# A scan of line convolutions: border products with 96 weight columns, side by side, and another order of products

## The chip, the cores and the metric

The kernel runs on one core of one Trainium2 chip. The metric is the device time of one execution in microseconds (us). A core has five engines that run side by side: TensorE (PE in the profile; its weight loads are listed apart as PEld), VectorE (DVE), ScalarE (ACT), GpSimd (POOL) and SyncE (SP), which here issues most of the DMA transfers.

## What is computed

The input x has 32 images of 48 channels, 64 rows and 128 columns, in float32. Two layers are applied, each `x = x + scan(groupnorm(x))`. The scan goes over the image four times: down the rows, up the rows, right over the columns, left over the columns. Each of its steps takes the line before it, convolves it along the line with 5 taps (48 channels to 48), adds a bias and adds the result to the line at hand:

```
def step(w, b):
    def f(carry, inp):
        nxt = inp + _conv1d(carry, w, b)   # 5 taps, padding 2
        return (nxt, nxt)
    return f
...
x = x + _L0_conv_ref(_gn(x), ...)
x = x + _L1_conv_ref(_gn(x), ...)
```

Each step needs the one before it. Group normalisation uses 16 groups of 3 channels over the whole image.

## The kernel before

**Layout.** A line is cut into blocks of 8 positions. A block has 8 x 48 = 384 values, channel by position, which lie on partitions as three groups of 128: group 0 holds positions 0, 1 and two thirds of 2; group 1 the rest of 2, then 3, 4 and a third of 5; group 2 the rest of 5, then 6 and 7. The table `PIECES` (line 50) tells where each piece lies: position, first and last channel, group, first partition. The free dimension holds block and image: 8 images at a time, 16 blocks in a row of 128 (128 columns of data). In a column scan two groups of images are taken together, again 128 columns.

**A step** (`step`, line 664) is nine products, listed in `PRODUCTS` (line 63) as input group, output group, and shift by a block. Seven stay in the block. Two are border products: (2, 0, -1) takes the last positions of the block before into group 0, and (0, 2, 1) the first positions of the block after into group 2. Their data is shorter by a block: 120 columns in a row scan, 112 in a column scan. Every product uses a 128 x 128 piece of the weight tile. Each of the three output groups has its own PSUM tile with one buffer; as soon as its last product is issued, a `scalar_tensor_tensor` on VectorE (line 684) adds the bias and the input line and writes the new line, which the next step's products read. A float32 product is two weight loads and two matmuls for TensorE.

**Phases.** `PHASES` (line 75) is the order of work: eight row phases of 126 steps (63 down, 63 up), one for each layer and group of 8 images, and four column phases of 254 steps (127 right, 127 left), each for two groups: 2024 steps in all. Row results go to DRAM (`ups`, by `move_rows`, line 528) and come back as columns (`load_unit`, line 572), in quarters of the width. A column phase of layer 0 adds the residual, keeps the result in DRAM and gathers statistics for the next layer; one of layer 1 adds the residual, permutes and stores the output, three quarters of it by way of the DRAM tiles `held` (`hold_result`, `let_result`, line 658).

**What sets the order.** Nothing is left to a scheduler: `in_order` chains the instructions of each engine in the order of the program. An agenda (`at`, `spread`) holds all side work with a due step, and `catch_up` emits what is due ahead of each step. On an engine's queue, side work therefore stands between steps. SP's queue holds nearly all transfers (line 200) and runs ahead of the steps where nothing makes it wait.

**Weights.** `load_weights` (line 232) puts the five taps in DRAM (`taps`), clears the weight tile and fills it with one transfer for each of the ten pieces, 5 x 48 columns wide. It is called six times: once in the first group's work, and at steps 176 and 180, 556, 1188 and 1192 by the agenda, whose transfers SP issues earlier.

**The start.** `first_group` (line 955) is written out by hand: loads of the first images in two parts, `take(0, b)` and `take(1, b)`, two transfers each; between them `let_go(n)` releases n of the transfers that were held back (an identity, the weights, masks and biases). The statistics of the last part lead to the scale of the first rows and so to the first step.

Of the kernel before, what the change touches and what calls it, by code (L numbers as in the profile page):

```python
# [33 lines left out]
C = 48  # L34
ODD = 64
P = ODD + C
TAPS = 5
# [5 lines left out]
E8 = 8  # L43
FULL = 128
NG = E8 * C // FULL
# [4 lines left out]
PIECES = (  # L50
    (0, 0, 48, 0, 0),
    (1, 0, 48, 0, 48),
    (2, 0, 32, 0, 96),
    (2, 32, 48, 1, 0),
    (3, 0, 48, 1, 16),
    (4, 0, 48, 1, 64),
    (5, 0, 16, 1, 112),
    (5, 16, 48, 2, 0),
    (6, 0, 48, 2, 32),
    (7, 0, 48, 2, 80),  # L60
)

PRODUCTS = (
    (0, 0, 0),
    (0, 1, 0),
    (1, 0, 0),
    (1, 1, 0),
    (2, 0, -1),
    (2, 1, 0),
    (1, 2, 0),  # L70
    (0, 2, 1),
    (2, 2, 0),
)

PHASES = (
    ("rows", 0, 0),
# [15 lines left out]
def kernel(  # L92
# [11 lines left out]
    NH = H // E8  # L104
# [29 lines left out]
    def const(shape, name):  # L134
# [9 lines left out]
    wt = {  # L144
        k: early[:, i * WEIGHTS : (i + 1) * WEIGHTS].rearrange("p (i n) -> p i n", i=NG)
        for i, k in enumerate(("down0", "down1", "right"))
    }
# [51 lines left out]
    def dma(dst, src, queue=None):  # L199
        (queue or nc.sync).dma_start(dst, src)  # L200
# [31 lines left out]
    def load_weights(key: str, layer: int, way: int, dma=dma):  # L232


        t = taps[layer][way]
        for j in range(TAPS):
            d, si = divmod(TAPS - 1 - j, 2)
            dma(t[:, j], w[SIDES[si], layer, way, d, SIDES[0]])
        nc.gpsimd.memset(wt[key], 0.0)
        for e, c0, c1, i, p0 in PIECES:  # L240
            to = C * (e - TAPS // 2) - FULL * (i - 1)
            dma(
                wt[key][p0 : p0 + c1 - c0, i, to : to + TAPS * C],
                t[c0:c1].rearrange("c k m -> c (k m)"),
            )

    def load_constants(dma):
# [391 lines left out]
    def in_output(j, g, e):  # L639


        t = out[g * GB : (g + 1) * GB].rearrange("b c (a e) w -> e (c a) b w", e=E8)
        return t[e, :, :, j * WQ : (j + 1) * WQ]
# [14 lines left out]
    def let_result(j, half, e):  # L658

        src = held[j, half].rearrange("o p (a b n) -> (o p a) b n", a=NH, b=GB)  # L660
        dma(in_output(j, half, e), src[e * C * NH : (e + 1) * C * NH])


    def step(key, weights, b_at, src, inp, dst, whole, part):


        ps = [
            ps_step.tile([FULL, N], F32, tag=f"step{o}", name=f"step{o}_{key}")
            for o in range(NG)
        ]  # L670
        left = [sum(1 for p in PRODUCTS if p[1] == o) for o in range(NG)]
        seen = [0] * NG
        for i, o, s in PRODUCTS:
            seen[o] += 1
            nc.tensor.matmul(  # L675
                part(whole(ps[o]), -s),
                weights[:, i, FULL * (o - NG * s - i + 1) : FULL * (o - NG * s - i + 2)],
                part(src(i), s),
                start=seen[o] == 1,
                stop=seen[o] == left[o],  # L680
            )
            if seen[o] == left[o]:
                layer, way = b_at
                nc.vector.scalar_tensor_tensor(  # L684
                    dst(o),
                    whole(ps[o]),
                    bd[:, o, layer, way : way + 1],
                    inp(o),
                    ALU.add,
                    ALU.add,  # L690
                )

    def row_step(k, h, prev, inp, name):
        _, layer, g = PHASES[k]

        def part(t, s):
            return t[:, max(0, s) * GB : N + min(0, s) * GB]

        step(
            f"{layer}{g}{name}{h}",  # L700
            wt[f"down{layer}"],
            (layer, DOWN),
            lambda i: prev[:, i],
            lambda o: inp[:, o],
            lambda o: row(k, h)[:, o],
            lambda ps: ps,
            part,
        )

    def col_step(k, way, v0, v1):  # L710
        _, layer, pair = PHASES[k]

        def col(v):
            kb, e = divmod(v, E8)
            j, kk = divmod(kb, KQ)
            view = slot[slots(k)[j % 3]].rearrange(
                "p (o m e k b) -> p o e k m b", o=NG, e=E8, k=KQ, b=GB
            )
            return lambda o: view[:, o, e, kk]

        def part(t, s):
            t = t.rearrange("p (s a) b -> p s a b", s=2)
            return t[:, :, max(0, s) : NH + min(0, s)] if s else t

        step(
            f"{layer}{pair}{'drl'[way]}{v1}",
            wt["right" if way == RIGHT else "left"],
            (layer, way),
            col(v0),
            col(v1),  # L730
            col(v1),
            lambda ps: ps.rearrange("p (m b) -> p m b", b=GB),
            part,
        )
# [87 lines left out]
    def plan_cols(k, t0, prev):  # L822
# [83 lines left out]
        if layer and not final:  # L906
            todo = [(j, half, e) for j in HELD for half in range(2) for e in range(E8)]
            for n, what in enumerate(todo):
                at(end + 63 + 1.9 * n, let_result, *what)
# [35 lines left out]
    def more_weights(key, layer, way):  # L945
        load_weights(key, layer, way)
# [8 lines left out]
    def first_group():  # L955
# [5 lines left out]
        def let_go(n):  # L961
            for _ in range(min(n, len(later))):
                dma(*later.pop(0))
# [18 lines left out]
        for b in range(2 * GB):  # L982
# [3 lines left out]
            i, b = divmod(b, GB)  # L986
            (nc.vector if b % 2 else nc.gpsimd).memset(parts[i][32:64, b], 0.0)

        def take(i, b):
            for s in range(2):  # L990
                take_batch(0, b, i * HALF + s * rows, s, parts[i])
# [15 lines left out]
        def rows_by_product(h0, n):  # L1007
            src = parts[0][0:C].rearrange("p b (r k e) -> p e r k b", k=NK, e=E8)
            for o in range(NG):
                ps = ps_rows.tile([FULL, n * N], F32, tag=f"rows{o}", name=f"rows{o}_{h0}")  # L1010
                mine = [(e, m) for m, (e, _, _, g, _) in zip(to_row, PIECES) if g == o]
                for i, (e, m) in enumerate(mine):
                    nc.tensor.matmul(
                        ps.rearrange("p (r k b) -> p r k b", r=n, b=GB),
                        m,
                        src[:, e, h0 : h0 + n],
                        start=i == 0,
                        stop=i == len(mine) - 1,
                    )
                nc.scalar.copy(  # L1020
                    row_views(0)[0][:, o, h0 : h0 + n],
                    ps.rearrange("p (r n) -> p r n", n=N),
                )
# [3 lines left out]
        for b in range(1, 3):  # L1027
            take(0, b)
        load_weights("down0", 0, DOWN, hold)
        load_constants(hold)  # L1030
        for b in range(3, GB):
            let_go(3)
            take(0, b)
        for b in range(4):
            let_go(3)
            take(1, b)
        for b in range(GB):
            stats.take(0, parts[0], b)
# [3 lines left out]
            put_row(0, r)  # L1042
        for b in range(4, GB):
            take(1, b)
            let_go(5)
        rows_by_product(0, 4)
        rows_by_product(4, 4)
        for r in range(12, 16):
# [32 lines left out]
        take_in(1, 0, nats1[0])  # L1081

    in_order(first_group)
    at(starts[0] + 10, scale_rows, 0, 40, 48)
    for j in range(1, 4):
# [71 lines left out]
```

## Time and profile before

| what | value |
|---|---|
| median of 3 runs | 4360.81 us (4360.26 to 4363.12) |
| span of the profiled execution, its own time | 4362.4 us |
| TensorE matmul / weight load busy | 4148.9 us / 4119.6 us |
| VectorE / ScalarE / GpSimd busy | 2178.5 / 1337.5 / 887.7 us |
| matmuls, weight loads | 36624 each |
| DMA moved | 680.34 MB in 2112607 packets |
| first step's first weight load | 96.6 us |
| last matmul ends | 4283.2 us |

A line of the groups reads: line of the kernel, engine, operation, written tile <- read tiles, shapes, count | busy us, mean ns of one | idle time of the engine before them and what ended it. A line of the time line reads: start in us, length in us, engine, line, operation, tiles, shapes, count, and in brackets the idle time before it. A line of the stretches reads: from and to in us, length, then the busy time and count on TensorE, weight load, VectorE, ScalarE and GpSimd, then the granted TensorE clock, the mean busy share of the 16 DMA engines (overlapping packets can bring it above 1) and GB/s. The shape `128*112` behind a matmul or weight load is rows of the array by weight columns; a matmul's `128x112` is its data.

### The profile page before, as it was taken

Reading aid. Unit: us, or ns where it says so; the run is one execution under the profiler, and the core shown is the slowest. Engines: PE = TensorE matmul, PEld = TensorE weight load, DVE = VectorE, ACT = ScalarE, POOL = GpSimd, SP = SyncE. Lnnn points to the kernel's source line nnn. Section 1 sums busy time; section 2 is a strip of 40 time slices with the busy share of each in tenths; the row PEclk is TensorE's granted clock in tenths of the full one; section 3 lists DMA queues with packets and bytes.
Section 4 is the critical chain, followed back from the end, with each engine's and each line's share of the span. In section 5 each row is a group of like instructions: output and inputs, shape, how many; then the busy total and the mean of one; then the engine's idle time right before and its main releaser. Section 6 shows DMA issues by size and latency. Waiting matters only on the chain. (4 is left out here: it accounts for less than half of the span.)

```text
span 4362.4 us, 90034 instructions
## 1 busy us (share of the span) xinstructions
PE 4148.9 (95%) x36624; PEld 4119.6 (94%) x36624; DVE 2178.5 (50%) x6554; ACT 1337.5 (31%) x2656; POOL 887.7 (20%) x859
## 2 busy tenths in 40 slices
PE   4898999998999999999999999999999999999992
PEld 2898999998999999999999999999999999999992
DVE  6344444446665444444446665444444444444443
ACT  2583301435795545100006774503000012110122
POOL 4561011324322020010004310000000024410352
PEclk9999999999999999999999999999999999999996
DMA  9999799866998989579407989839288049999999
GB/s 191 171 192 163 111 155 164 217 128 198 231 200 149 157 160 157 91 127 195 85 1 239 227 166 141 127 59 163 37 140 184 1 82 245 236 240 156 172 199 180
DMA packets 2112607, 680.34 MB, mean 156 GB/s; under 512 B 2000448, under 2 KB 2052032, under 8 KB 2072256
## 3 DMA queue, kind: packets, MB, share of 16 engines
q1 hardware_dynamic: 2014176, 582.29, 70.3%
q10 hardware_dynamic: 94816, 86.00, 9.7%
q0 software_dynamic: 3200, 6.30, 0.6%
q8 instruction: 288, 4.72, 0.5%
q14 instruction: 127, 1.04, 0.1%
HBM read 397.57 MB, written 295.99 MB: 159 GB/s over the span
## 5 line engine op out<-in xcount | busy, mean ns | idle before, releaser
L553 ACT ACTIVATE arena<-arena,offset,scale 128x256 f32<-128x256 f32 (+2 forms) x816 | 577.0, 801 | 413.5 <-DMA arena<-mid 160.9
L612 POOL TENSOR_TENSOR arena<-arena 128x2048 f32<-128x2048 f32 x80 | 362.8, 4550 | 1504.4 <-PE step_10l L675 452.9
L510 POOL COPY arena<-arena 112x256 f32<-112x256 f32 x458 | 271.1, 653 | 553.3 <-DMA arena<-in_x 298.9
L675 PE MATMUL step_00r<-arena,early 128*128 128x128 f32 x2286 | 259.0, 277 | 15.4 <-DMA arena<-upa 15.2
L675 PEld LDWEIGHTS step_00r<-arena,early 128*128 128x128 f32 x2286 | 258.3, 194 | 16.1 <-issue 15.5
L675 PE MATMUL step_01r<-arena,early 128*128 128x128 f32 x2286 | 258.5, 277 | 14.3 <-DMA arena<-upa 14.3
L675 PEld LDWEIGHTS step_01r<-arena,early 128*128 128x128 f32 x2286 | 258.1, 193 | 14.7 <-issue 14.4
L675 PE MATMUL step_11r<-arena,early 128*128 128x128 f32 x2286 | 258.5, 276 | 5.9 <-DVE arena L684 5.9
L675 PEld LDWEIGHTS step_11r<-arena,early 128*128 128x128 f32 x2286 | 257.8, 193 | 6.5 <-DVE arena L684 6.2
L444 ACT ACTIVATE early<-arena 128x256 f32<-128x256 f32 x192 | 129.3, 674 | 426.8 <-PE step_01l L675 328.7
L675 PE MATMUL step_00l<-arena,wleft 128*128 128x128 f32 x2286 | 257.9, 276 | 0.0
L675 PEld LDWEIGHTS step_00l<-arena,wleft 128*128 128x128 f32 x2286 | 257.5, 193 | 0.0
L675 PE MATMUL step_10r<-arena,early 128*128 128x128 f32 x2286 | 256.1, 275 | 0.0
L675 PEld LDWEIGHTS step_10r<-arena,early 128*128 128x128 f32 x2286 | 255.7, 192 | 0.3
L675 PE MATMUL step_11l<-arena,wleft 128*128 128x128 f32 x2286 | 255.8, 275 | 0.0
L675 PEld LDWEIGHTS step_11l<-arena,wleft 128*128 128x128 f32 x2286 | 255.5, 192 | 0.2 <-DVE arena L684 0.2
L675 PE MATMUL step_01l<-arena,wleft 128*128 128x128 f32 x2286 | 255.7, 275 | 0.0
L675 PEld LDWEIGHTS step_01l<-arena,wleft 128*128 128x128 f32 x2286 | 255.5, 192 | 0.1
L675 PE MATMUL step_10l<-arena,wleft 128*128 128x128 f32 x2286 | 255.5, 275 | 0.0
L675 PEld LDWEIGHTS step_10l<-arena,wleft 128*128 128x128 f32 x2286 | 255.4, 192 | 0.0
L637 ACT COPY arena<-arena 128x256 f32<-128x256 f32 x172 | 99.5, 656 | 414.0 <-POOL arena L612 166.7
L377 ACT ACTIVATE early<-arena 112x512 f32<-112x512 f32 x192 | 121.1, 631 | 298.2 <-DMA arena<-in_x 227.2
(176 smaller groups left out, 7117.1 us busy)
## 6 DMA issues: line engine op xcount, KB each, us to landing
arena<-in_x SPq DMA_DIRECT2D x48, 768.0 KB, 12.8
xin<-arena SPq DMA_DIRECT2D x96, 384.0 KB, 5.5
arena<-xin SPq DMA_DIRECT2D x96, 384.0 KB, 8.1
mid<-arena SPq DMA_DIRECT2D x96, 384.0 KB, 7.8
arena<-mid SPq DMA_DIRECT2D x192, 192.0 KB, 4.4
upb<-arena SPq DMA_DIRECT2D x192, 192.0 KB, 3.9
arena<-upb SPq DMA_DIRECT2D x96, 384.0 KB, 11.9
arena<-xin SPq DMA_DIRECT2D x186, 192.0 KB, 4.3
```

Source lines behind the costliest of these rows:

```text
L377: nc.scalar.activation(junk[0:P], piece, AF.Identity, accum_out=self.sum[:, at[0], at[1]],)
L444: nc.scalar.activation(junk[:, 0:n], view[:, b], AF.Identity, accum_out=self.sum[:, i, j : j + 1])
L510: copy(dst[:, r, q], src[:, r0 + r, q])
L553: nc.scalar.activation(args[0], args[0], AF.Identity, bias=args[2], scale=args[1])
L612: eng.tensor_tensor(unit, unit, nat, ALU.add)
L637: copy(by_w(perm)[:, a], src[:, a])
L675: nc.tensor.matmul(part(whole(ps[o]), -s), weights[:, i, FULL * (o - NG * s - i + 1) : FULL * (o - NG * s - i + 2)], part(src(i), s), star ...
```

## The change

Group 2 now holds positions 6 and 7 on partitions 0 to 95 and the two thirds of position 5 behind them. What a border product writes then lies on the first 96 partitions in both directions (positions 0 and 1 of group 0, 6 and 7 of group 2), and it uses 96 weight columns and the first 96 partitions of its PSUM tile. The two border products are the third and fourth of a step, and the order of the others is different. As the positions of group 2 are no longer in ascending order, a piece's weights aren't one run of columns: `weight_runs` works the runs out, 25 in place of 10, with a transfer for each. The results of positions 2 and 5 are let go in two transfers each, where one served: 60 in place of 48. At the start, `let_go` releases 4 and 7 transfers at a time in place of 3 and 5.

```diff
-    (5, 16, 48, 2, 0),
-    (6, 0, 48, 2, 32),
-    (7, 0, 48, 2, 80),
+    (6, 0, 48, 2, 0),
+    (7, 0, 48, 2, 48),
+    (5, 16, 48, 2, 96),
 )
 PRODUCTS = (
     (0, 0, 0),
+    (2, 2, 0),
+    (0, 2, 1),
+    (2, 0, -1),
+    (1, 0, 0),
+    (1, 2, 0),
     (0, 1, 0),
-    (1, 0, 0),
     (1, 1, 0),
-    (2, 0, -1),
     (2, 1, 0),
-    (1, 2, 0),
-    (0, 2, 1),
-    (2, 2, 0),
 )
+BORDER = 2 * C
+def weight_runs():
+    runs = []
+    for e, c0, c1, i, p0 in PIECES:
+        mine = []
+        for tap in range(TAPS):
+            t, q = divmod(e + tap - TAPS // 2, E8)
+            for qe, m0, m1, g, q0 in sorted(PIECES):
+                if qe == q:
+                    mine.append((tap * C + m0, FULL * (g + NG * t - i + 1) + q0, m1 - m0))
+        at, to, n = mine[0]
+        for a, b, m in mine[1:]:
+            if (a, b) == (at + n, to + n):
+                n += m
+            else:
+                runs.append((c0, c1, i, p0, at, to, n))
+                at, to, n = a, b, m
+        runs.append((c0, c1, i, p0, at, to, n))
+    return runs
+WEIGHT_RUNS = weight_runs()
@@ load_weights
-        for e, c0, c1, i, p0 in PIECES:
-            to = C * (e - TAPS // 2) - FULL * (i - 1)
+        for c0, c1, i, p0, at, to, n in WEIGHT_RUNS:
             dma(
-                wt[key][p0 : p0 + c1 - c0, i, to : to + TAPS * C],
-                t[c0:c1].rearrange("c k m -> c (k m)"),
+                wt[key][p0 : p0 + c1 - c0, i, to : to + n],
+                t[c0:c1].rearrange("c k m -> c (k m)")[:, at : at + n],
             )
@@ let_result
-        dma(in_output(j, half, e), src[e * C * NH : (e + 1) * C * NH])
+        for n, c0, c1, g, p0 in PIECES:
+            if n == e:
+                at = (g * FULL + p0) * NH
+                dma(in_output(j, half, e)[c0 * NH : c1 * NH], src[at : at + (c1 - c0) * NH])
@@ step
             seen[o] += 1
+            m = BORDER if s else FULL
+            at = FULL * (o - NG * s - i + 1)
             nc.tensor.matmul(
-                part(whole(ps[o]), -s),
-                weights[:, i, FULL * (o - NG * s - i + 1) : FULL * (o - NG * s - i + 2)],
+                part(whole(ps[o])[0:m], -s),
+                weights[:, i, at : at + m],
                 part(src(i), s),
@@ first_group
         for b in range(3, GB):
-            let_go(3)
+            let_go(4)
             take(0, b)
         for b in range(4):
-            let_go(3)
+            let_go(4)
             take(1, b)
...
             take(1, b)
-            let_go(5)
+            let_go(7)
```

## The prediction

> **What bounds the kernel now.** I read the page's shares first, then groups with shapes kept apart in an undisturbed stretch (700 to 900 us), then time lines around the few matmuls that are shaped otherwise, then the waits that interrupt the steps.
>
> ```profile
> span 4362.4 us, 90034 instructions
> PE 4148.9 (95%) x36624; PEld 4119.6 (94%) x36624; DVE 2178.5 (50%) x6554; ACT 1337.5 (31%) x2656; POOL 887.7 (20%) x859
> ...
> L675 PEld LDWEIGHTS step_00r<-arena,early 128*128 128x128 f32 x1785 | 199.7, 192 | 0.6 <-DVE arena L684 0.3
> L675 PE MATMUL step_00r<-arena,early 128*128 128x128 f32 x1390 | 191.1, 277 | 0.1
> L675 PE MATMUL step_00r<-arena,early 128*128 128x112 f32 x396 | 74.0, 268 | 0.0
> ```
>
> TensorE is never idle there. A product is two weight loads and two matmuls, a step has nine products: 18 pairs. 200 us / 1785 loads = 112 ns per load; the single records of the trace say 111.7 ns from load to load, without exception, and the median step is 18 x 111.7 = 2010 ns. 2024 steps x 2.010 = 4068 us; the rest is 96.6 us before the first step, 79 us after the last and 118 us of interruptions.
>
> Who sets 111.7, the load or the matmul? The border matmuls stream 112 columns in a column scan (120 in a row scan). In the single records the matmul behind one starts after 98 ns (105 in rows) instead of 112, then waits: the next load comes after 111.7 all the same. So around a border product the weight load binds, at 128 columns. Does a narrower load take less? The group averages answer:
>
> ```profile
> 1302.55 0.68 PEld L272 LDWEIGHTS ps_r<-mv_r_r,mask_in 128*112 128x112 f32 x6
> 1303.14 0.97 PEld L675 LDWEIGHTS step_02d<-arena,early 128*128 128x128 f32 x8
> ...
> 1307.16 0.75 PEld L276 LDWEIGHTS ps_r<-mean_c_r,maskp 112*128 112x128 f32 x6
> 1307.84 0.30 PEld L675 LDWEIGHTS step_02d<-arena,early 128*128 128x128 f32 x2
> ```
>
> Six loads of 112 weight columns take 0.59 us until the next line's load, six of 128 take 0.68. Singly: 98.3 against 111.7 ns, 13.4 ns for 16 columns, 0.84 ns a column. An estimate for 96 columns from these two: 98.3 - 13.4 = 84.9 ns. The first of the six still took 110 ns, since the matmul before it had 128 columns. A load begins when the previous pair's matmul begins; so the time from one load to the next is the longer of this load and the matmul of the pair before it.
>
> **The change, part by part.** *Border products with 96 columns, side by side.* Take the pairs X (full), b1, b2, b3, b4 (two border products), Y (full). After b1's load: 84.9 against X's matmul of 111.7, so 111.7. After b2, b3, b4: 84.9 against a border matmul of 98.3 (105 in rows), so 98.3 (105). After Y: 111.7 against 98.3, so 111.7. Three intervals of 18 shrink: 3 x 13.4 = 40.2 ns per column step, 3 x 6.7 = 20.1 per row step. Apart, each border product would give one interval. Bounds: nothing, if 96 columns load like 128; four intervals (53.6 and 26.8), if Y's load also starts early. I take three, by the group-average rows.
>
> A rule would give far more: the Trainium skill, "TensorE: Matmul & The Clock Gate", section "Back-to-back issue gap", has an isolated matmul occupy N/2.4 + 2.5 ns, 49 ns for 112 columns. Then loads alone would bind: four intervals x 26.8 = 107 ns a step, 217 us in all, about 4144 us. The row here is 98 ns from one float32 matmul's start to the next; the measurement decides, and I stay with 40.2 and 20.1.
>
> *Order of products.* Output groups now end after products 5 (group 0), 6 (group 2) and 9 (group 1) and are first read by products 1, 2 and 5 of the next step. Before: 5, 6, 9, where the group of 6 had to be out of its PSUM tile by product 2. The distances are the same, four products each, only the last has two border products inside it.
>
> ```profile
> 1012.38 0.61 DVE L684 SCALAR_TENSOR_TENSOR arena<-step_00l,bd,arena 128x128 f32<-128x128 f32 x2 [0.75 <-PE step_00l L675]
> 1013.28 0.35 DVE L684 SCALAR_TENSOR_TENSOR arena<-step_00l,bd,arena 128x128 f32<-128x128 f32 x1 [0.30 <-PE step_00l L675]
> ```
>
> From the last matmul's start 314 ns to VectorE's start, 350 of work, 50 to the waiting load: 714 ns, where eight intervals and a little (896) are there. Measured over all steps the median slack is 193, 157 and 182 ns for the three results; the last falls to 182 - 40 = 142. No wait, so zero; without that cover each missing ns would come back 2024 times.
>
> *Moved partitions.* Ten pieces and ten transfers per group as before: zero in all stores and loads, which SP issues. Two exceptions. A weight load needs 25 transfers in place of 10, six times, and letting the held results go needs 60 in place of 48: 102 more on SP's queue, at 0.45 us by
>
> ```profile
> 472.37 4.50 SPq L200 DMA_DIRECT2D early<-taps  x10
> ```
>
> 46 us of issue if nothing covered it. Later it is covered: behind the weights of 472 and 492 us SP next waits for rows from VectorE (27.2 us of waiting from 498 to 560); behind those of 2584 its loads are due some 60 steps later; the held results end at 4058, the next store goes out at 4099. At the start it is not: 15 more stand ahead of the last image (`let_go` 4 and 7 for 3 and 5), and its statistics lead the first step.
>
> ```profile
> 0.00:100.00 100.00, 43.44 (x70) 18.65 (x71) 66.89 (x100) 17.60 (x35) 41.55 (x65) 1.00 0.97 188
> ```
>
> The DMA share (0.97) is full; packets of 960 B took 100 ns, of 192 B 33 ns, so 624 more packets add about 0.7 us on 16 engines and 15 completions 0.3: lower bound 1 us. Upper: 15 x 0.45 = 7 us if SP is the limit. SP mostly waits for earlier images here (29.9 us), so nearer the lower: +2.5.
>
> *What the saving meets.* It doesn't arrive where something else ends the wait.
>
> ```profile
> L684 DVE SCALAR_TENSOR_TENSOR arena<-step_01d,bd,arena 128x128 f32<-128x128 f32 x9 | 3.0, 349 | 17.2 <-DMA arena<-xin 14.3 <-PE step_01d L675 2.1 <-ACT arena L553 0.8
> ...
> 3899.05 0.35 DVE L684 SCALAR_TENSOR_TENSOR arena<-step_11r,bd,arena 128x128 f32<-128x128 f32 x1 [6.55 <-DMA arena<-upb]
> ...
> 4220.00:4260.00 40.00, 39.96 (x357) 39.77 (x357) 19.14 (x60) 10.13 (x18) 25.90 (x17) 1.00 1.21 188
> 4260.00:4300.00 40.00, 23.22 (x208) 23.02 (x207) 23.67 (x45) 8.55 (x15) 18.52 (x17) 0.82 1.24 191
> ```
>
> Step 142 waits at 422 us for rows that the DMA engines, full since the start, bring: the first 142 row steps give nothing. At 3899 (step 1834) the third quarter is late, its loads released at step 1801: 33 x 40 ns = 1.3 us more waiting. From 4100 on (step 1933) the DMA share stays above 1.1 to the end: the last 91 column steps give nothing. Around step 540 ScalarE's scaled rows come 2 to 4 us ahead with the DMA full; from 451 the steps gain 3.2: 1.0 us lost.
>
> Sum: (1016 - 91) x 40.2 = 37.2 us; (1008 - 142) x 20.1 = 17.4; together 54.6. Against it 2.5 + 1.3 + 1.0 = 4.8. Profile: 4362.4 - 49.8 = 4312.6. The profiled span lies 1.6 above the median of the runs (4360.8), so **4311**.
>
> **Rivals.** *Four intervals* (0.09): the records show a load 16 ns behind its matmul's start after a border, so some slack is passed on; 54.6/3 = 18.2 more, 4293. Against: the load spacing never moved from 111.7. *Two intervals, or DMA takes a third back* (0.09): 4329; for it, the DMA share is above 0.95 in over a third of the 100 us stretches; against, late data stops the steps only at 16, 32, 142 and 1834. *Nothing* (0.08): 96 columns load like 128; 4361 + 2.5 = 4363. Against: 98.3 for 112. *Slower* (0.08): the array drains whenever the number of active columns changes. The Trainium skill, "TensorEngine Tiling (Array Packing)", section "Key Properties", says that changing the tiling mode drains TensorE; 112 columns still reach into the fourth 32, 96 do not, so the row that shows no drain between 112 and 128 (98 ns into the full load at 1303.14) doesn't exclude it. A drain bares what a 275 ns matmul hides, 163 ns, twice a step: 326 - 30, x 2024, near 4960 us; from some 13 ns per change on it decides. [...]
>
> **How the numbers follow.** The likeliest case (0.66) is 4311, its own range 4302 (start and losses near zero, part of the first 142 steps kept) to 4323 (start 7, one later weight load uncovered). The range adds four intervals below and two above: 4290 to 4342, holding 0.66 + 0.09 + 0.09, less a little. About 0.2% (8.7 us) can be told from no change. Faster: 0.66 + 0.18 = 0.84, of which I keep 0.83; same 0.08; slower 0.09.
>
> **What would show it.** Right: load spacings of 98 and 105 three times a step, steps of 1970 and 1990 ns; loads of 96 columns near 165 ns; first step near 99 us; the wait at step 142 longer by about 2 us, at 1834 by 1; a tail longer by 3 to 4. Wrong: spacings of 111.7 (nothing), above 112 (drain), or VectorE waits at the head of each step.

## The result, and the profile after

The changed kernel takes 4321.68 us (median of 4 runs, 4318.79 to 4327.19), the kernel before 4361.97 us beside it (4 runs, 4360.26 to 4368.4): a ratio of 0.9906, 95% interval 0.9892 to 0.992. The forecast was 4311 with a range of 4290 to 4342: the direction and the range held, and 40.3 us came where 49.8 were worked out. The small gap hides two larger ones, one on each side.

The head of the page of the changed kernel:

```profile
span 4325.4 us, 89999 instructions
...
PE 4072.9 (94%) x36624; PEld 4042.5 (93%) x36624; DVE 2177.4 (50%) x6554; ACT 1337.2 (31%) x2656; POOL 891.9 (21%) x859
```

The number of matmuls and loads is the same, and TensorE's busy time fell by 76 us, twice as much as the span (37.0 us). So the steps gained more than the span shows, and idle time grew. Both halves can be read. First the steps: groups of weight loads and matmuls with shapes kept apart, from 2000 to 2200 us. In the kernel before there is one group of loads:

```profile
L675 PEld LDWEIGHTS step_01r<-arena,early 128*128 128x128 f32 x1788 | 200.0, 192 | 0.2
```

and in the changed kernel:

```profile
L706 PEld LDWEIGHTS step_01r<-arena,early 128*128 128x128 f32 x1431 | 167.9, 192 | 0.0
L706 PEld LDWEIGHTS step_01r<-arena,early 128*96 128x96 f32 x408 | 47.4, 164 | 0.0
L706 PE MATMUL step_01r<-arena,early 128*128 128x128 f32 x1432 | 178.1, 276 | 0.0
L706 PE MATMUL step_01r<-arena,early 128*96 128x112 f32 x408 | 55.8, 259 | 0.0
```

Loads of 96 columns last 164 ns from issue to end, where those of 128 last 192; there is no idle time between them. The count gives the step: 1839 loads in 200 us, where the kernel before has 1788. From the single records the median step is 1960 ns in column scans and 1980 in row scans, before 2010 in both. The saving is 50 and 30 ns a step, forecast 40.2 and 20.1: 1016 x 50 + 1008 x 30 = 81.0 us over the whole kernel, where 61.1 would have followed from the forecast's figures.

Then the idle time. I split each profiled execution at the first step's first load and into the scans' phases, and took the time above "number of steps x the phase's median step" as waiting (us):

| part | before | after | more |
|---|---|---|---|
| up to the first step | 96.6 | 109.1 | 12.5 |
| waits, steps 0 to 505 (three phases) | 78.3 | 82.6 | 4.3 |
| waits, fourth phase, from step 506 | 5.3 | 17.8 | 12.5 |
| waits, eighth phase, from step 1138 | 5.1 | 12.8 | 7.7 |
| waits, last phase | 9.6 | 11.8 | 2.2 |
| waits, other phases | 20.1 | 19.9 | -0.2 |
| after the last step | 79.2 | 84.3 | 5.1 |
| sum | | | 44.1 |

81.0 - 44.1 = 36.9 us, against 37.0 between the two spans. More than half of the step time won is given back in waits here. The profiled execution is the slowest of the changed kernel's four, 5.5 us above their median; by the medians 40.3 of the 81.0 us came through, so about half was given back.

The two largest have their lines. In the stretches of the start, 60 to 80 us, the DMA share (the figure before the last) is 0.98 with the kernel before and 0.82 with the changed one:

```profile
60.00:80.00 20.00, 14.31 (x16) 4.29 (x14) 11.22 (x20) 3.04 (x4) 10.86 (x26) 1.00 0.98 212
```

```profile
60.00:80.00 20.00, 19.06 (x21) 5.89 (x20) 8.53 (x15) 2.65 (x5) 10.86 (x26) 1.00 0.82 188
```

In the fourth phase, the time line of SP's queue, of ScalarE and of VectorE in the changed kernel:

```profile
1325.13 12.48 SPq L227 DMA_DIRECT2D early<-taps  x25
...
1342.80 2.84 SPq L227 DMA_DIRECT2D arena<-in_x  x2
...
1358.89 0.63 ACT L403 ACTIVATE early<-arena 112x512 f32<-112x512 f32 x1 [21.07 <-DMA arena<-in_x]
...
1371.83 0.21 ACT L344 ACTIVATE std_r<-var_r 128x24 f32<-128x24 f32 x1
...
1372.07 0.30 DVE L348 RECIPROCAL std_r<-std_r 128x24 f32<-128x24 f32 x1 [9.85 <-ACT std_r L344]
```

and the same stretch in the kernel before:

```profile
1327.76 4.75 SPq L200 DMA_DIRECT2D early<-taps  x10
...
1339.75 1.19 SPq L200 DMA_DIRECT2D arena<-in_x  x2
...
1353.24 0.63 ACT L377 ACTIVATE early<-arena 112x512 f32<-112x512 f32 x1 [13.52 <-DMA arena<-in_x]
...
1366.18 0.20 ACT L318 ACTIVATE std_r<-var_r 128x24 f32<-128x24 f32 x1
...
1366.63 0.29 DVE L322 RECIPROCAL std_r<-std_r 128x24 f32<-128x24 f32 x1
```

Read from top to bottom: 25 weight transfers hold SP's queue 12.48 us in place of 4.75; the images behind them go out 3.05 us later, though the weights began 2.6 us earlier; ScalarE's sixteen passes over these images begin 5.65 us later; the standard deviation that VectorE's row normalisation wants stands on ScalarE behind those sixteen, so VectorE waits 9.85 us, and with it the `scalar_tensor_tensor` whose line the next step's matmuls need. Step 591 starts 9.6 us late. In the kernel before the same deviation was ready 0.25 us ahead of its use (1366.38 against 1366.63 us): there was hardly a margin, and nothing in a table of busy shares says so.

### The profile page after: what moved, and what is told of

Read it like the earlier page. It is cut to its first block, busy times and chain, and to the rows that moved or that the text cites. A ratio compares the mean times of both kernels' runs of the same rounds, so it can differ in the third digit from the quotient of the medians.

```text
span 4325.4 us, 89999 instructions
## 1 busy us (share of the span) xinstructions
PE 4072.9 (94%) x36624; PEld 4042.5 (93%) x36624; DVE 2177.4 (50%) x6554; ACT 1337.2 (31%) x2656; POOL 891.9 (21%) x859
## 5 line engine op out<-in xcount | busy, mean ns | idle before, releaser
L706 PE MATMUL step_00r<-arena,early 128*128 128x128 f32 x2286 | 252.4, 274 | 15.3 <-DMA arena<-upa 14.2
L706 PEld LDWEIGHTS step_00r<-arena,early 128*128 128x128 f32 x2286 | 251.9, 187 | 15.8 <-issue 15.8
```

What stands on the lines that cost most here:

```text
L706: nc.tensor.matmul(part(whole(ps[o])[0:m], -s), weights[:, i, at : at + m], part(src(i), s), start=seen[o] == 1, stop=seen[o] == left[o],)
```

## The experiments

Two questions were open. Does the step follow the rule "the longer of this load and the matmul of the pair before", with only its figures off? And do the waits come from the extra transfers, or from steps that now run ahead of what feeds them? Beside these four kernels the kernel before took 4361.06 us (median of 7 runs, 4353.1 to 4367.38).

**All new pieces, transfers and orders, but loads of 128 columns.**

```
-BORDER = 2 * C
+BORDER = FULL
```

> The changed kernel with 128 weight columns again in the border products (side by side, new order, new pieces and transfers all kept). Theory (narrow loads give the gain): steps of 2010 ns, no shorter interval; the time is the changed kernel's plus its 50 x 1016 + 30 x 1008 ns = 81 us, less what the waits give back, 4375 to 4403, above the kernel before by the new transfers alone. Rival (order or neighbourhood gives the gain): near 4322.

Measured: 4378.55 us (4372.95 to 4382.47), ratio 1.0042, interval 1.0027 to 1.0057: slower than before by 17.5 us. Groups from 2000 to 2200 us:

```profile
L706 PEld LDWEIGHTS step_01r<-arena,early 128*128 128x128 f32 x1792 | 200.2, 192 | 0.0
L706 PE MATMUL step_01r<-arena,early 128*128 128x128 f32 x1393 | 173.4, 276 | 0.0
L706 PE MATMUL step_01r<-arena,early 128*128 128x112 f32 x400 | 59.6, 272 | 0.0
```

The steps are back at 2010 ns in both scans, with 1792 loads in 200 us. So standing side by side and the other order are worth nothing alone; the 96 columns are the whole gain, and what the change brings besides costs 17.5 us in the medians. The profiled execution, the fastest of its four, shows 8.8 us of them: first step at 103.4 (+6.8), fourth phase +11.4, the first three phases -5.5, the end -3.5, each other phase between -1.1 and +0.9. At step 591 the same chain stands:

```profile
1331.44 12.84 SPq L227 DMA_DIRECT2D early<-taps  x25
...
1365.09 0.63 ACT L403 ACTIVATE early<-arena 112x512 f32<-112x512 f32 x1 [21.24 <-DMA arena<-in_x]
...
1378.26 0.30 DVE L348 RECIPROCAL std_r<-std_r 128x24 f32<-128x24 f32 x1 [8.86 <-ACT std_r L344]
```

No step is faster here, and step 591 is still 8.6 us late. In the three kernels below, all with 25 transfers at this place, it is 6.8 to 9.9 us late, and in the kernel before not at all. So the wait does not come from steps that run ahead. That the longer turn of the weights on SP's queue makes it is read from the lines; a kernel with all else changed but 10 transfers here was not run.

**The two border products apart.**

```
 PRODUCTS = (
     (0, 0, 0),
+    (2, 0, -1),
     (2, 2, 0),
     (0, 2, 1),
-    (2, 0, -1),
     (1, 0, 0),
```

> The changed kernel with the second and third product swapped in the list so that a full product stands between the two border products, 96 columns kept. Theory (an interval is the longer of a load and of the matmul of the pair before): each border product alone has one short interval, not three for two: steps of about 1974 (columns) and 1987 ns (rows), 22 us more than the changed kernel, near 4343. Rival (each narrow load gains by itself): steps stay at 1960 and 1980, near 4322.

The edit moves the fourth product of the changed kernel to the second place, which puts (2, 2, 0) between the two border products. Measured: 4326.72 us (4318.62 to 4328.09), ratio 0.992, interval 0.9906 to 0.9935; steps of 1973 ns in column scans and 1987 in row scans. Its loads from 2000 to 2200 us, 1826 for the changed kernel's 1839:

```profile
L706 PEld LDWEIGHTS step_01r<-arena,early 128*128 128x128 f32 x1421 | 174.6, 192 | 0.0
L706 PEld LDWEIGHTS step_01r<-arena,early 128*96 128x96 f32 x405 | 55.5, 164 | 0.0
```

The intervals from load to load in the records around each border product are 110.7, 95.9, 110.0 (columns) and 110.7, 102.4, 110.0 (rows), all others 111.7: one short interval for a border product that stands alone, three for two that stand together, as the rule has it. The steps cost 1016 x 13 + 1008 x 7 = 20.3 us more than in the changed kernel, the medians differ by 5.0, and the ranges overlap. In the profiled executions, this kernel's fastest against the changed kernel's slowest, the one with the products apart is even the shorter by 8.7 us: its first step came 6.3 us earlier, its waits were 18.3 us fewer, its end 4.3 us shorter. So the steps show what standing together wins, but the times of the two kernels can't be told apart; by the medians three quarters of it are lost in waits.

**Border loads of 112 columns, side by side.**

```
-BORDER = 2 * C
+BORDER = 112
```

> The changed kernel with 112 weight columns in the border products. Theory: a load of 112 columns takes 98.3 ns, longer than the column scan's matmul (96.0) and shorter than the row scan's (102.7): column steps near 1967, row steps unchanged at 1980 ns, 7 us more than the changed kernel, near 4329. Rival (loads alone set the interval): rows grow as well; other rival (anything under 128 is the same): near 4322.

Measured: 4325.6 us (4319.56 to 4327.71), ratio 0.9919, interval 0.9905 to 0.9934; steps of 1968 and 1980 ns. Its groups from 2000 to 2200 us:

```profile
L706 PEld LDWEIGHTS step_01r<-arena,early 128*112 128x112 f32 x404 | 48.9, 178 | 0.0
...
L706 PE MATMUL step_01r<-arena,early 128*112 128x112 f32 x404 | 56.0, 261 | 0.0
```

In column scans the short intervals are 96.7, 98.3 and 98.3 ns, where the changed kernel has 95.9, 95.9 and 95.8. So with 112 columns the load binds (98.3, as the small loads of the kernel before had it), and with 96 columns the matmul binds: 95.9 ns for 112 data columns. In row scans, with 120 data columns, both kernels have 102 to 103: the matmul binds in either. This separates the two terms that the forecast had set equal. Narrowing the load below 112 columns wins 8 ns a column step and nothing in rows.

**The 25 weight transfers of the start on ScalarE's queue.** The held transfers carry their queue with them, and those left to SP are let go in the rounds of the kernel before.

```
             dma(
                 wt[key][p0 : p0 + c1 - c0, i, to : to + n],
                 t[c0:c1].rearrange("c k m -> c (k m)")[:, at : at + n],
+                nc.scalar if key == "down0" else None,
             )
...
-            let_go(4)
+            let_go(3)
...
-            let_go(7)
+            let_go(5)
```

> The changed kernel with the first weights' 25 transfers issued from ScalarE's queue and the held transfers let go by 3 and 5 as before. Theory (the 15 extra transfers take SP's turns ahead of the images): first step at 96 to 99 us instead of 109, about 10 to 12 us less in all, near 4310. Rival (the DMA engines are full, it doesn't matter who issues): first step stays above 105, near 4321.

Measured: 4319.67 us (4313.58 to 4321.92), ratio 0.9905, interval 0.9888 to 0.9922, not to be told from the changed kernel; first step at 106.6 us. The stretches of its start and ScalarE's queue:

```profile
40.00:60.00 20.00, 18.90 (x22) 6.15 (x21) 5.32 (x9) 7.21 (x12) 4.66 (x8) 1.00 0.60 106
60.00:80.00 20.00, 16.96 (x19) 5.21 (x17) 10.29 (x18) 3.04 (x4) 8.54 (x15) 1.00 1.02 233
```

```profile
33.39 18.67 ACTq L227 DMA_DIRECT2D early<-taps  x25
```

```profile
SPq L227 <- DMA early<-taps: 8.1, 6, 4.6
```

From 60 to 80 us the DMA engines are full again, but from 40 to 60 their share is only 0.60. ScalarE issues 25 transfers in one go of 18.67 us, and SP itself waits 8.1 us for six of them: a transfer on the other queue still holds up SP here. The loss moved 20 us forward and stayed. My expectation of a start like the kernel before's was wrong; the rival's numbers came (above 105, near 4321), but not for its reason, as the DMA engines were not full from 40 to 60 us. The single records say why ScalarE's queue was no way out: its transfers and SP's take the same eight semaphores in one rotation. SP's image transfer at 49.39 us, for one, starts when ScalarE's transfer on the same semaphore, issued at 44.50, has landed at 49.38. ScalarE's own copies, which begin at 39.7 us in the kernel before, stand behind its 25 transfers and begin at 52.1. A queue with semaphores of its own was not tried.

## Why the prediction was near, and where it was not

**The rule of the step held, its matmul term was mis-sized.** "After b2, b3, b4: 84.9 against a border matmul of 98.3 (105 in rows)": three short intervals came, at these places and no others, but the matmul takes 95.9 and 102.6 ns. I had read 98.3 and 105 off the start of the matmul behind a border matmul, whose own load was 128 columns wide; the value is not the border matmul's. With 128 columns in the changed order the two starts are again 98.3 and 105.0 ns apart, in both scans 2.4 ns more than with 96; why the wide load adds that stays open. The load figure of 98.3 for 112 columns was right, as the kernel with 112 columns shows. The intervals at the edges, forecast at 111.7, are 110.9 (narrow load behind a full matmul) and 110.0 (full load behind a border matmul). Column step: 3 x 15.8 + 0.8 + 1.7 = 49.9 ns, measured 50. This term alone was 19.9 us too small.

**No drain, and no short occupancy.** The drain that the Trainium skill, "TensorEngine Tiling (Array Packing)", section "Key Properties", states for a change of tiling mode would have shown where 128 columns meet 96: the records have 110.9 ns into the border and 110.0 out of it, less than 111.7. Whether 96 columns change the mode at all, no run here shows. The 49 ns by the occupancy rule of the Trainium skill, "TensorE: Matmul & The Clock Gate", section "Back-to-back issue gap", is excluded too: with loads of 96 columns, estimated at 84.9, the interval stops at 95.9, so it is the matmul that fills it. Both times built on them, 4960 and 4144, are out. So are the other counts of intervals: a fourth short one would stand where the edges show 110.0 and 110.9, two would stand where three are, and "nothing" is the kernel with 128 columns.

**The order of products cost nothing,** as forecast: the median slack of the third result is 151 ns in the records, forecast 142, and only one in a hundred is below 131. The stretch from 2900 to 3000 us shows TensorE's loads without a gap:

```profile
2900.00:3000.00 100.00, 100.00 (x911) 100.00 (x910) 48.59 (x152) 36.10 (x48) 0.00 (x0) 1.00 0.92 138
```

**"Later it is covered" failed.** The step looked for waits of SP behind the weights of 472, 492 and 2584 us and found slack. It never followed the third weight load, near step 556 (1325 us), where images stand behind the 25 transfers, sixteen ScalarE passes behind the images, and a standard deviation with a margin of 0.25 us behind the passes. Cost: 8.6 us with the steps unchanged, 9.6 in the changed kernel.

**"SP mostly waits for earlier images here, so nearer the lower: +2.5" failed.** The first step came at 109.1; the four kernels with the same start code have 102.8, 103.4, 106.9 and 109.1, so the cost is 6 to 12 us against the one profile of the kernel before, at and above the upper bound of 7. Why is seen in the time line of SP's queue, not in a busy share. The last two pairs of images in the kernel before:

```profile
69.92 0.89 SPq L200 DMA_DIRECT2D arena<-in_x  x2
...
73.75 1.17 SPq L200 DMA_DIRECT2D arena<-in_x  x2
```

and in the changed kernel, with the first of the seven small transfers behind the pair at 72.97 us:

```profile
73.79 0.42 SPq L227 DMA_DIRECT2D bd<-in_b  x1
...
79.95 0.78 SPq L227 DMA_DIRECT2D arena<-in_x  x2
...
86.80 0.78 SPq L227 DMA_DIRECT2D arena<-in_x  x2
```

The last pair goes out at 86.80 us in place of 73.75. The records show SP's transfers taking 8 semaphores in rotation, and never more than 8 under way: each waits for the landing of the one eight places ahead (the image at 79.95 us starts when the one issued at 73.32 has landed, at 79.94). With 5 small transfers and 2 images in a round (before), the next two images go out while at least one of the last two is still landing. With 7 and 2 a round is nine, and the records show no image under way when the next are issued, at 73.0, 80.0 and 86.8 us; small transfers issued behind images mostly take 5 to 6 us to land, like the images, and move little meanwhile. That fits the share of 0.82. That the rounds of nine do it, and not the 15 transfers as such, is argued from these records alone; rounds of 5 throughout in the changed kernel, and rounds with 7 in the kernel before, were not tried. That the last kernel above, with its 5 and 2 on SP, has the share back at 1.02 from 60 to 80 us speaks for it.

**"What the saving meets" came near in size, in part by luck.** The first 142 row steps gave next to nothing, as forecast: from the first step to step 142 it is 326.1 us before and 325.4 after (323.0 with 128 columns, so the figure varies by some us without faster steps). The wait at step 142 grew by 2.1 us (15.5 for 13.4; forecast about 2), but it is 6.7 us in the kernel with 128 columns and 8.1 in the one with 112, whose row steps are as fast as the changed kernel's, so 2 us can't be put down to the steps. At step 555 there is a new wait of 1.3 us, forecast 1.0 near step 540 because the steps run ahead; the kernel with 128 columns, where no step is faster, has it too, with 1.3 us. That number was luck. At step 1834 the wait for the third quarter was 6.55 us and is now

```profile
3865.93 0.61 DVE L715 SCALAR_TENSOR_TENSOR arena<-step_11r,bd,arena 128x128 f32<-128x128 f32 x2 [8.72 <-DMA arena<-upb]
```

2.2 us more, forecast 1.3; but it is 7.6 with 128 columns and 4.9 with the products apart, so the lead of the steps is not shown to be the cause. The end is longer by 5.1 us, forecast 3 to 4: over six profiles it is 75.7 and 79.2 us with column steps of 2010 ns, 80.0 with 1973 and 82.1 to 84.4 with 1968 or less, which fits the forecast's reason. One reading of the prediction was wrong as well: late data stops the steps not at four places alone. The groups of the kernel before put 15.2 and 14.3 us of TensorE's idle time at the heads of layer 0's two column phases (steps 252 and 884) down to the DMA `arena<-upa`; with the change they are shorter by less than 1 us.

Not seen at all were the waits of the eighth phase, 7.7 us more, the longest of them at steps 1170 and 1186:

```profile
2536.45 0.35 DVE L715 SCALAR_TENSOR_TENSOR arena<-step_11d,bd,arena 128x128 f32<-128x128 f32 x1 [2.27 <-ACT arena L579]
...
2571.51 0.35 DVE L715 SCALAR_TENSOR_TENSOR arena<-step_11d,bd,arena 128x128 f32<-128x128 f32 x1 [3.01 <-ACT arena L579]
```

VectorE waits for rows that ScalarE scales late. With steps of 2010 ns this phase has 5.1 and 6.0 us of waits, with 1987 it has 7.1; with 1980 it has 12.8 in two kernels and 7.4 in a third. Faster steps alone don't settle it; what else decides there stays open.

**The sum by cause.** The forecast had 52.3 us for the narrow loads with the waits that they meet (54.6 - 1.3 - 1.0) and a cost of 2.5 for the transfers. The medians give 4378.55 - 4321.68 = 56.9 for the narrow loads and 17.5 for the rest of the change. The net miss of some 10 us is thus the rest, 15.0 us dearer than priced, less 4.6 us from the loads. That the loads came so near is partly luck: the steps saved 19.9 us more than forecast (81.0 for 61.1), and waits took 15.3 us more of it (24.1 for 8.8). The second half of the rival "Two intervals, or DMA takes a third back" therefore came true in size, 24.1 of 81.0 us, though no run shows that DMA alone took them. A version that loads the third group of weights behind the images of step 591 was not tried.

## What to carry to other kernels

Where loads and matmuls overlap, measure each one's interval where it binds: the start of a matmul behind another was 2.4 ns more here than the interval that the matmul set once the load was short. A saving spread over thousands of steps pays only down to the margin of everything that feeds the steps; here about 57 of 81 us came through. Price added DMA issues at each place they are issued, by following what stands behind them on the queue to the consumer with the least margin, and count how many can be under way at once, over all queues that share their semaphores.

## What the runs showed of the hardware that was not expected

- A float32 pair's interval is bound by the load at 111.7 ns for 128 weight columns and 98.3 for 112, and by the matmul at 95.9 ns for 112 data columns and 102.6 for 120: at 112 columns the load is the longer by 2.4 ns.
- Changing between 96 and 128 weight columns costs nothing that the records show (110.0 and 110.9 ns).
- 25 transfers issued by ScalarE in place of SP took 0.75 us each (0.50 on SP near 1325 us) and held SP up by 8.1 us: with eight semaphores shared by both, a second queue was no way around the first one's waits.
- The same start code put the first step anywhere from 102.8 to 109.1 us in four profiled executions.
